# A four-layer kernel on one core: weights prepared in another order, the first image's values computed earlier, the second image's convolution inputs transformed once and kept in HBM

## The chip, the cores and the metric

The kernel runs on one core of a Trainium2 chip. The metric is the device time of one execution in microseconds. Of a core the reader needs TensorE (matmuls; a weight load goes before each), VectorE, ScalarE and GpSimd (elementwise work), and SyncE, which here only issues DMAs. They are PE, DVE, ACT, POOL and SP in the profile. Each engine takes its instructions in program order and they wait for each other by semaphores. TensorE writes to PSUM, which VectorE and ScalarE read; all else lies in SBUF, and DMAs move data between SBUF and HBM.

## What is computed

The input x is two images of 128 channels and 64 x 64 pixels, float32. Four layers follow each other:

```python
x = L0(x, ...)   # 1x1 embedding, two Mamba blocks (conv of 4 taps, scan over 4096 tokens, FFN), 1x1 out, + x
x = L1(x, ...)   # q, k, v = 3x3 convolutions of x; softmax(q.k / sqrt(C)) v over 4096 tokens; 1x1 out, + x
x = L2(x, ...)   # q, k, v = 1x1 convolutions; softmax(q.k) v; x + gamma * that
x = L3(x, ...)   # features at four scales, attention over the scales, layer norm, 1x1 fusion
```

The change touches the start of L0, and L1. Each image's L1 needs three 3x3 convolutions, for queries, keys and values, of the same input. They are done with a transform along the rows: out of six shifted views of a row, six combinations are made (they depend on the input alone), each is multiplied with a transformed weight, and four output columns come out of the six products.

## The kernel before

The activations of both images stay in SBUF as `xt`. L0 is cut into 32 items (image, block, chunk of 512 tokens), and each item into 32 slots. `slot` issues what belongs to the scan itself: the decay factors `da` (ACT, L377), the inputs of the scan `h` (DVE, `times_b`, L370), the scan (DVE, L388), the product with C (POOL, L391), the sum over states (PE, `y_pair`, L403), and the loads of `dtb` (`spread_dt`, SP, L359). `background` gives each slot its share of the matmuls and layer norms of the items before and after; its numbers are due slots, written by hand. Two rounds without a scan come first (items -2 and -1) and bring item 0 as far as the scan.

Before that stand the loads, all on SP in the order of the code: constants, eight chunks of the first image (L93), the embedding's weights, then for each of the two blocks its weights, the conv weights `cw` (L145, L146) and `wd`, then `raw`, the L1 convolution weights (L167), and the second image (L170). For each block VectorE makes `wu` (L152), and the table of decay rates `am` is made from `an` by four matmuls (L159) and 16 small copies (L162). The weights of L1 are transformed by `fold` (L172, ten VectorE operations for each of q, k and v), in slots 2, 10 and 18 of round -1, and stored to `ufold` in HBM. `spread_bc` (L327) sends an item's B and C through HBM (`dr`) and spreads them over partitions as `bb` and `cb`, all in slot 14.

L1 and L2 are one loop over `now`, 128 slots for each of four runs: L1 of both images, then L2 of both. A slot computes scores of 128 queries against 1024 keys (`score`, L725 on PE and L730 on DVE, which evicts them and takes maxima), and 14 slots later (`LAG`) four products of weights and values (`product`, L775). Between lie the exponentials (ACT, L740), a 32 x 32 block transpose (DVE, L755), and its rearrangement `pt<-tr`: 16 pieces a time, eight of them DMAs on SP (L766), four on ACT, four copies on POOL.

For L1, `inputs(r, cc)` (L587) makes the six combinations of a quarter of an image: twelve VectorE operations into `dlo` (four combinations, in the last part of the weight buffer `uw`) and `dhi` (two). `products_by` (L613) multiplies them with the transformed weights: 18 matmuls of 128 x 256, in six steps of three, one step for each combination. `outputs` (L634) makes the results: two ScalarE and nine VectorE operations. `beginning` runs the first image's queries (one quarter) and keys beside the last slots of L0; the string `beside` says how many of its steps stand in each slot. For the second image `keys` stands in front of its slot 0, and for both images `values` stands at the end of slot 13; both go through `chunks`, which calls `inputs` again for each quarter. `queries` of the other quarters stand at slot 30 of each 32, with `inputs` two operations a slot from slot 16 on. So each quarter of an image is transformed for queries, for keys and for values, apart from the quarters that are reused at once:

```python
pp = products(which)
ahead = inputs(r, cc + 1) if cc + 1 < NCC else []
for f in ahead[:8]:
    f()
outputs(*pp, [dst[:, i * QG : (i + 1) * QG] for i in range(4)], bias(r, which))
for f in ahead[8:]:
    f()
```

There is one `dlo` and one `dhi`: the next quarter's combination is written when the product that read the old one is done. L3, after the loop, is not touched.

Of the kernel before, what the change touches and what calls it, by code (L numbers as in the profile page):

```python
# [14 lines left out]
N = H * W  # L15
# [52 lines left out]
def tile_conv_seq(ctx: ExitStack, tc, x, consts, vecs, wemb, wlay, wconv, wdt, wqkv, wsmall, wms, out):  # L68
# [23 lines left out]
    for c in range(NCH):  # L92
        nc.sync.dma_start(xv(0, c), x[0, :, c * RPC : (c + 1) * RPC, :])  # L93

    ud = ctx.enter_context(tc.tile_pool(name="ufold", bufs=1, space=bass.MemoryType.DRAM))
    ufold = [ud.tile([P, 18, C], F32, name=f"ufold{k}") for k in range(3)]

# [16 lines left out]
    with tc.manual_schedule(), ExitStack() as s:  # L114
# [25 lines left out]
        wl, wu, wd, am = [], [], [], []  # L140
        for l in range(NL):
            w = wp.tile([P, NWL - DI], F32, name=f"wl{l}")
            nc.sync.dma_start(w, wlay[l][:, DI:])
            cw = sp.tile([P, KC + 1, DI], F32, name="cw", tag="h", bufs=5)
            nc.sync.dma_start(cw[:, :KC, :].rearrange("p k d -> p (k d)"), wconv[l : l + 1, :].to_broadcast([P, KC * DI]))  # L145
            nc.sync.dma_start(cw[:, KC, :], wlay[l][:, :DI])  # L146
            d = wp.tile([R, DI], F32, name=f"wd{l}")
            nc.sync.dma_start(d, wdt[l])

            u = wp.tile([P, KC, DI], F32, name=f"wu{l}")  # L150
            for k in range(KC):
                nc.vector.tensor_tensor(u[:, k, :], cw[:, KC, :], cw[:, k, :], ALU.mult)  # L152
            an = wp.tile([P, NJ * DS], F32, name=f"an{l}")
            nc.scalar.activation(an, vec[:, VEC[f"A_log{l}"] : VEC[f"A_log{l}"] + NJ * DS], AF.Exp)
            nc.vector.tensor_scalar(an, an, -1.0, None, ALU.mult)
            a = wp.tile([P, NJ, 4, 4], F32, name=f"am{l}")
            for g in range(4):
                pa = mm.tile([P, NJ, DS], F32, name="pa", tag="mm")
                nc.tensor.matmul(pa.rearrange("p j n -> p (j n)"), lhsT=four(g), rhs=an, start=True, stop=True)  # L159
                for q in range(4):  # L160
                    at = slice(32 * q, 32 * q + 32)
                    nc.vector.tensor_copy(a[at, :, g, :], pa[at, :, 4 * q : 4 * q + 4])  # L162
            wl.append(w), wu.append(u), wd.append(d), am.append(a)
        raws = []
        for which in range(3):
            raw = sp.tile([P, 3, 3, C], F32, name="raw", tag="h", bufs=5)
            nc.sync.dma_start(raw.rearrange("p y x c -> p (y x) c"), wqkv[:, which])  # L167
            raws.append(raw)
        for c in range(NCH):
            nc.sync.dma_start(xv(1, c), x[1, :, c * RPC : (c + 1) * RPC, :])  # L170
# [156 lines left out]
        def spread_bc(i):  # L327

            dr = dp.tile([2 * DS, CH], F32, name="dr", tag="dr")
            nc.sync.dma_start(dr, st[i]["dbl"][R:])  # L330
            for k in range(2):
                o = st[i]["bc", k] = sp.tile([P, 4, CH], F32, name=("bb", "cb")[k], tag=("bb", "cb")[k], bufs=2)
                for q in range(4):
                    src = dr[k * DS + 4 * q : k * DS + 4 * q + 4, :].rearrange("(o m) f -> o (m f)", o=1)
                    nc.sync.dma_start(o[32 * q : 32 * q + 32].rearrange("p m f -> p (m f)"), src.to_broadcast([32, 4 * CH]))
# [134 lines left out]
        def background(i):  # L470
# [14 lines left out]
            if has(n):  # L485
                at(0, pu_taps, n, 0, (0, 1)), at(1, pu_taps, n, 0, (2, 3)), at(2, pu_out, n, 0)
                at(3, pu_taps, n, 1, (0, 1)), at(4, pu_taps, n, 1, (2, 3)), at(5, pu_out, n, 1)
                at(13, xproj, n), at(14, xproj_out, n), at(14, spread_bc, n)
                at(15, dtproj, n, 0), at(16, dtproj, n, 1), at(17, soft_plus, n), at(18, dt_end, n)
# [5 lines left out]
            if i == -1:  # L495
                for k in range(3):
                    at(8 * k + 2, fold, k)
# [23 lines left out]
        def slot(i, todo, t_):  # L521
            t = i * NSL + t_
            g, m = divmod(t, 4)
            if m == 0 and 0 <= g + 3 < NG:
                spread_dt(g + 3)
            if m == 0 and 0 <= g + 1 < NG:
                spread_dtu(g + 1)
            if m == 0 and g % 2 == 1 and 0 <= g - 3 < NG:
                y_pair(g - 3)
            if 0 <= t < NT:  # L530
                scan(t)
            if 0 <= t + 4 < NT:
                decay(t + 4)
            if m == 3 and 0 <= g + 1 < NG:
                times_b(g + 1)
            for f, a in todo[t_]:
                f(*a)
# [75 lines left out]
        def products_by(which):  # L613
# [3 lines left out]
            for slot, dst in enumerate((pa[:, 2, :], pa[:, 0, :], pa[:, 3, :], pa[:, 1, :], pb[:, 0, :], pb[:, 1, :])):  # L617
                d = dlo[:, slot] if slot < 4 else sta["dhi"][:, slot - 4]
                for y in range(3):
                    rhs = d[:, y : y + 16, :].rearrange("p h j -> p (h j)")  # L620
                    lhsT = uw[:, where[which, slot // 3], 3 * (slot % 3) + y, :]
# [35 lines left out]
        def chunks(r, which, to):  # L657

            for cc in range(NCC):
# [6 lines left out]
                else:  # L666
                    pp = products(which)
                    ahead = inputs(r, cc + 1) if cc + 1 < NCC else []
                    for f in ahead[:8]:
                        f()  # L670
                    outputs(*pp, [dst[:, i * QG : (i + 1) * QG] for i in range(4)], bias(r, which))
                    for f in ahead[8:]:
                        f()
# [4 lines left out]

        def values(r):
            vt = sta["vt"] = sp.tile([P, N // P, C], F32, name="vt", tag="vt")  # L680
            vs = {}

            def turned(cc):
                for i in range(2):
                    pt = psa.tile([P, 4, P], F32, name="pvt", tag="acc")
                    for a in range(4):
                        at = (4 * i + a) * P
                        nc.tensor.transpose(pt[:, a, :], vs[cc][:, at : at + P], ident)
                    at = (2 * cc + i) * 4
                    nc.scalar.copy(vt[:, at : at + 4, :], pt)  # L690
# [129 lines left out]
        LO, HI = 0, 1  # L820
        def beginning():

            for which, half in ((0, LO), (0, HI), (1, LO)):
                load(which, half)
            for f in inputs(0, 0):
                f()
# [6 lines left out]
            k = sta["k"] = spa.tile([P, N], F32, name="k", tag="k")  # L833
            for cc in range(NCC):
                pp = yield from products_by(1)
                ahead = inputs(0, cc + 1) if cc + 1 < NCC else []
                for f in ahead[:8]:
                    f()
                at = cc * 4 * QG
                outputs(*pp, [k[:, at + i * QG : at + (i + 1) * QG] for i in range(4)], bias(0, 1))  # L840
# [5 lines left out]
        beside = '2111001000112111111011010000'  # L846
# [6 lines left out]
        for _ in steps:  # L853
            pass
        layers.close()
# [3 lines left out]
        for now in range(NALL + LAG + 10):  # L859
            r, u = divmod(now, NU)  # L860
            w = now % 8
            if now < NALL:
# [11 lines left out]
                if now >= 16 and r4 < B:  # L874
                    if v == 0:
                        ahead = inputs(r4, cc)
                    if v < 6:
                        for f in ahead[2 * v : 2 * v + 2]:
                            f()
                    if v == 14:  # L880
                        queries(r4, cc)
                        if r4 and cc == 0:
                            load(1, HI)
                score(r, u)
# [3 lines left out]
                elif u == 1:  # L888
                    load(2, LO), load(2, HI)
                    first = inputs(r, 0)  # L890
                elif 6 <= u < 12:
                    for f in first[2 * u - 12 : 2 * u - 10]:
                        f()
# [21 lines left out]
            if now < NALL and u == LAG - 1:  # L915
# [457 lines left out]
```

## Time and profile before

| | us |
|---|---|
| median of 3 runs | 5076.93 (5076.55 to 5080.12) |
| the profiled execution | 5077.7 |
| its span in the profile | 5075.9 |
| first scan starts | 84.94 |
| last scan ends, about | 2104 |
| first score of the attention (slot 0 of run 0) | 2189.1 |
| first score of slot 14 of run 0 | 2272.9 |
| first score of run 1 (L1, second image) | 2752.8 |
| first score of run 2 (L2, first image) | 3292.6 |
| last score | 4244.2 |

The times in the table are starts from the span's beginning. In the profile a line such as L725 is a line of the kernel; `out<-in` are the program's names; "idle before" is the time that the engine stood still just before an instruction, with what ended it. The granted clock is the share of TensorE's full clock: it is 1.00 or 0.50 at any moment, and a mean between them over a window.

The DMA issues that matter, from the page: each row is a group, with its queue, count, size and the median time from issue to landing.

| DMA | queue | count | KB | us |
|---|---|---|---|---|
| pt<-tr | SP | 2048 | 64 | 2.0 |
| dtb<-dt | SP | 1024 | 64 | 2.0 |
| bb<-dr | SP | 128 | 256 | 4.6 |
| cb<-dr | SP | 128 | 256 | 7.6 |
| uw<-ufold | SP | 14 | 576 | 3.7 |
| xt<-in_x | SP | 16 | 256 | 5.0 |
| xr<-in_x | SP | 16 | 256 | 2.9 |

### The profile page before, as it was taken

The numbers are of one execution on the slowest core, as the hardware profiler recorded it, in microseconds if no ns is written. First come the engines' busy times: TensorE is split into PE (matmuls) and PEld (weight loads), VectorE is DVE, ScalarE is ACT, GpSimd is POOL, SyncE is SP. The second block draws the span as 40 slices with busy tenths as digits, with TensorE's granted clock in tenths as the row PEclk, the third lists the DMA queues.
The fourth block names the chain that finished last, engine by engine and source line by source line (L and its number), as shares of the span: only waits on it lengthen the run. The fifth ranks groups of instructions, "written<-read, shape, count | busy, mean of one in ns | idle before, by whom it ended". The sixth has DMA issues, their size and how long they took to land.

```text
span 5075.9 us, 48999 instructions
## 1 busy us (share of the span) xinstructions
PE 4683.8 (92%) x14797; PEld 2250.9 (44%) x14797; DVE 4097.5 (81%) x4416; ACT 2366.9 (47%) x3221; POOL 2316.3 (46%) x1948
## 2 busy tenths in 40 slices
PE   5889999999988899889999999999999999999997
PEld 1222222222222222356666666666666666333332
DVE  5999999999999999788888878667766775667775
ACT  4677777777777777522222222333333332323332
POOL 2777776766777777413332233233333332322331
PEclk8898889988999989899999999999999999999998
DMA  5333333333333333124443344444444443000000
GB/s 149 72 69 68 70 71 70 72 69 68 69 70 68 72 72 71 46 54 102 105 102 84 77 104 103 118 97 111 111 100 99 112 111 77 5 5 7 7 7 7
DMA packets 237016, 373.86 MB, mean 74 GB/s; under 512 B 88000, under 2 KB 88400, under 8 KB 228432
## 3 DMA queue, kind: packets, MB, share of 16 engines
q1 hardware_dynamic: 187600, 303.55, 25.8%
q10 hardware_dynamic: 49152, 67.17, 5.8%
q8 instruction: 118, 1.93, 0.2%
q14 instruction: 146, 1.20, 0.1%
HBM read 92.18 MB, written 9.83 MB: 20 GB/s over the span
## 4 chain that ended last, share of the span: by engine, by line
PE 47%; POOL 21%; DVE 13%; issue 11%; DMA 3%; ACT 3%; SPq 2%; ACTq 0%; DVEq 0%; POOLq 0%
POOL h L391 16%; PE po L775 13%; PE pq L725 13%; DVE tr L755 3%; DMA pt<-tr 2%; PE pf L1060 2%; SPq L766 2%; PE py L403 2%; PE pqkv L1087 2%; PE pu L292 1%; PE pw L1146 1%; POOL dtu L351 1%; PE pfus L1211 1%; POOL z L414 1%; PE psc L1111 1%
## 5 line engine op out<-in xcount | busy, mean ns | idle before, releaser
L762 POOL COPY pt<-tr 32x512 f32<-32x512 f32 x1024 | 656.1, 641 | 1468.2 <-DVE tr L755 738.8
L388 DVE TENSOR_TENSOR_SCAN h<-da,carry,h 128x512 f32<-128x512 f32 x1024 | 1241.4, 1266 | 60.4 <-ACT da L377 31.6
L391 POOL TENSOR_TENSOR h<-h,cb 128x2048 f32<-128x2048 f32 x256 | 1161.1, 4536 | 20.8 <-POOL carry L390 0.2
L725 PE MATMUL pq<-k,q 128*128 128x512 f32 x2048 | 965.1, 594 | 11.2 <-DVE sc L730 8.8
L775 PE MATMUL po<-pt,vt 128*128 128x256 f32 x4096 | 967.5, 380 | 2.4 <-DMA pt<-tr 2.4
L740 ACT ACTIVATE sc<-sc,nm 128x2048 f32<-128x2048 f32 x256 | 510.6, 1995 | 937.2 <-DVE nm L736 641.7
L730 DVE TENSOR_SCALAR_CACHE_REDUCE sc<-pq 128x1024 f32<-128x1024 f32 x512 | 624.9, 1222 | 359.8 <-PE pq L725 337.9
L775 PEld LDWEIGHTS po<-pt,vt 128*128 128x128 f32 x4096 | 780.5, 191 | 293.9 <-issue 211.1
L377 ACT ACTIVATE da<-dtb,am 128x512 f32<-128x512 f32 x1024 | 681.7, 684 | 222.1 <-DVE h L388 210.6
L755 DVE STREAM_TRANSPOSE tr<-sc 128x2048 f32<-128x2048 f32 x256 | 591.6, 2311 | 65.8 <-DMA pt<-tr 60.5
L370 DVE TENSOR_TENSOR h<-bb,pdu 128x2048 f32<-128x2048 f32 x256 | 581.7, 2272 | 77.4 <-PE py L403 29.3
L403 PE MATMUL py<-h,sel 128*32 128x512 f32 x2048 | 511.5, 643 | 1.6 <-POOL h L391 1.6
L725 PEld LDWEIGHTS pq<-k,q 128*128 128x128 f32 x2048 | 384.5, 191 | 289.5 <-issue 247.1
L364 PE MATMUL pdu<-dtu,fsel 128*128 128x512 f32 x512 | 326.5, 724 | 101.9 <-DVE h L370 101.8
L403 PEld LDWEIGHTS py<-h,sel 128*32 128x32 f32 x2048 | 115.7, 118 | 415.9 <-issue 408.9
L292 PE MATMUL pu<-xn,wu 128*128 128x512 f32 x512 | 246.2, 615 | 3.0 <-ACT xn L282 2.1
L364 PEld LDWEIGHTS pdu<-dtu,fsel 128*128 128x128 f32 x512 | 96.2, 215 | 308.3 <-DVE h L370 187.6
L390 POOL COPY carry<-h 128x4 f32<-128x4 f32 x256 | 47.5, 185 | 388.1 <-DVE h L388 383.5
L1153 DVE TENSOR_TENSOR ov<-v,pw 128x2048 f32<-128x2048 f32 x64 | 146.2, 2285 | 68.5 <-PE pw L1146 68.5
L1087 PE MATMUL pqkv<-f,ws 128*128 128x512 f32 x384 | 189.7, 619 | 3.0 <-DVE prod L1104 2.3
L1157 POOL TENSOR_TENSOR ov<-ov 128x2048 f32<-128x2048 f32 x16 | 72.6, 4537 | 257.6 <-DVE ov L1153 257.6
L351 POOL TENSOR_TENSOR dtu<-dt,u 128x1024 f32<-128x1024 f32 x32 | 75.0, 2345 | 189.7 <-ACT dt L345 189.7
(241 smaller groups left out, 5344.1 us busy)
## 6 DMA issues: line engine op xcount, KB each, us to landing
pt<-tr SPq DMA_DIRECT2D x2048, 64.0 KB, 2.0
dtb<-dt SPq DMA_DIRECT2D x1024, 64.0 KB, 2.0
pt<-tr ACTq DMA_DIRECT2D x1024, 64.0 KB, 2.2
bb<-dr SPq DMA_DIRECT2D x128, 256.0 KB, 4.6
cb<-dr SPq DMA_DIRECT2D x128, 256.0 KB, 7.6
uw<-ufold SPq DMA_DIRECT2D x14, 576.0 KB, 3.7
xt<-in_x SPq DMA_DIRECT2D x16, 256.0 KB, 5.0
xr<-in_x SPq DMA_DIRECT2D x16, 256.0 KB, 2.9
```

Of the source, the lines that this page charges most:

```text
L364: nc.tensor.matmul(pdu, lhsT=four(s_ % 4), rhs=st[i]["dtu"][:, s_ // 4, :], start=True, stop=True)
L370: nc.vector.tensor_tensor(h, st[i]["bc", 0], pdu.unsqueeze(1).to_broadcast([P, 4, CH]), ALU.mult)
L377: nc.scalar.activation(da, st[i]["dtb", s_], AF.Exp, scale=am[items[i][1]][:, j, gg, m : m + 1])
L388: nc.vector.tensor_tensor_scan(h[:, m, :], da, h[:, m, :], carries[b, l][:, j, gg, m : m + 1], ALU.mult, ALU.add)
L391: nc.gpsimd.tensor_tensor(h, h, st[i]["bc", 1], ALU.mult)
L403: nc.tensor.matmul(py[r : r + 32, :], lhsT=sel, rhs=st[i]["h", s_ + k][:, m, :], start=(m == 0), stop=(m == 3), tile_position=(0, r),)
L725: nc.tensor.matmul(pq[:, i, :], lhsT=sta["q", r, grp][:, it * P : (it + 1) * P], rhs=sta["k"][:, at : at + CH], start=True, stop=True)
L730: nc.vector.tensor_scalar(dst, pq, 1.0, None, ALU.mult, ALU.max, accum_out=sta["mx"][:, c2 : c2 + 1])
L740: nc.scalar.activation(sc, sc, AF.Exp, bias=nm, scale=scale, accum_out=sm[:, hh : hh + 1])
L755: nc.vector.transpose(tr, sta.pop(("sc", r, blk, hh)).rearrange("p (t r f) -> p r t f", r=NB, f=32))
L762: nc.gpsimd.tensor_copy(dst, src)
L775: nc.tensor.matmul(sta["po", r, grp], lhsT=sta["vt"][:, jt, :], rhs=rhs, start=(jt == 0), stop=(jt == N // P - 1))
```

## The change

It has three parts.

The start: one chunk of the first image is loaded, then the first block's weights with `cw` ahead, then the other chunks and the second block. `prepare` makes a block's `am` ahead of its `wu`; that of the second block moves to slot 7 of round -1, the loads of `raw` and of the second image are issued in slot 1 of it, and the three folds stand in slots 8, 9 and 10. `cb` is spread in slot 22 instead of 14. The first `spread_dtu` and `times_b` get slots 19 and 26 of that round.

The values of the first image: `beginning` computes them beside the keys, from the same combinations, quarter by quarter, with their weights in a buffer of their own (`uv`). They are turned into `vt` in slots 0 to 3 of run 0 (`turned`). The block at slot 13 remains for the second image alone.

The second image: during run 0 its quarters are transformed in slots 32, 64 and 96 (and the first one from slot 112 on, as before), and `keep` stores each to HBM, `dkept`. For keys, values and queries of run 1, `fetch` loads a quarter back in three DMAs on SP, one for each two combinations, in place of the twelve operations.

```diff
-    for c in range(NCH):
-        nc.sync.dma_start(xv(0, c), x[0, :, c * RPC : (c + 1) * RPC, :])
+    def load_x(b, c):
+        nc.sync.dma_start(xv(b, c), x[b, :, c * RPC : (c + 1) * RPC, :])
...
+    dkept = [ud.tile([P, 6, 18 * 16], F32, name=f"dkept{k}") for k in range(4)]
...
-        wl, wu, wd, am = [], [], [], []
-        for l in range(NL):
+        load_x(0, 0)
+        wl, wu, wd, am, cws = [], [], [], [], []
+
+        def load_layer(l):
+            cw = sp.tile([P, KC + 1, DI], F32, name="cw", tag="h", bufs=5)
+            nc.sync.dma_start(cw[:, KC, :], wlay[l][:, :DI])
+            nc.sync.dma_start(cw[:, :KC, :].rearrange("p k d -> p (k d)"), wconv[l : l + 1, :].to_broadcast([P, KC * DI]))
+            cws.append(cw)
             w = wp.tile([P, NWL - DI], F32, name=f"wl{l}")
...
-            cw = sp.tile([P, KC + 1, DI], F32, name="cw", tag="h", bufs=5)
-            nc.sync.dma_start(cw[:, :KC, :].rearrange("p k d -> p (k d)"), wconv[l : l + 1, :].to_broadcast([P, KC * DI]))
-            nc.sync.dma_start(cw[:, KC, :], wlay[l][:, :DI])
...
-            u = wp.tile([P, KC, DI], F32, name=f"wu{l}")
-            for k in range(KC):
-                nc.vector.tensor_tensor(u[:, k, :], cw[:, KC, :], cw[:, k, :], ALU.mult)
+            wl.append(w), wd.append(d)
+
+        def prepare(l):
             an = wp.tile([P, NJ * DS], F32, name=f"an{l}")
...
-            wl.append(w), wu.append(u), wd.append(d), am.append(a)
+
+            u, cw = wp.tile([P, KC, DI], F32, name=f"wu{l}"), cws[l]
+            for k in range(KC):
+                nc.vector.tensor_tensor(u[:, k, :], cw[:, KC, :], cw[:, k, :], ALU.mult)
+            wu.append(u), am.append(a)
...
+        def load_rest():
...
+            for c in range(NCH):
+                load_x(1, c)
+
+        load_layer(0)
+        load_x(0, 1)
+        prepare(0)
+        for c in range(2, NCH):
+            load_x(0, c)
+        load_layer(1)
...
-        def spread_bc(i):
...
+        def spread_bc(i, k):
+
+            if k == 0:
+                st[i]["dr"] = dp.tile([2 * DS, CH], F32, name="dr", tag="dr")
+                nc.sync.dma_start(st[i]["dr"], st[i]["dbl"][R:])
+            dr = st[i]["dr"]
...
-                at(13, xproj, n), at(14, xproj_out, n), at(14, spread_bc, n)
+                at(13, xproj, n), at(14, xproj_out, n), at(14, spread_bc, n, 0), at(22, spread_bc, n, 1)
...
             if i == -1:
+                at(1, load_rest), at(7, prepare, 1)
                 for k in range(3):
-                    at(8 * k + 2, fold, k)
+                    at(8 + k, fold, k)
+                at(19, spread_dtu, 0), at(26, times_b, 0)
...
-            if m == 0 and 0 <= g + 1 < NG:
+            if m == 0 and 1 <= g + 1 < NG:
...
-            if m == 3 and 0 <= g + 1 < NG:
+            if m == 3 and 1 <= g + 1 < NG:
...
-        def products_by(which):
+        def keep(cc):
+            nc.sync.dma_start(dkept[cc][:, :4, :], dlo.rearrange("p s y j -> p s (y j)"))
+            nc.sync.dma_start(dkept[cc][:, 4:, :], sta["dhi"].rearrange("p s y j -> p s (y j)"))
+
+        def fetch(cc):
+            dhi = sta["dhi"] = spa.tile([P, 2, 18, 16], F32, name="dhi", tag="d")
+            for k, d in enumerate((dlo[:, :2], dlo[:, 2:], dhi)):
+                nc.sync.dma_start(d.rearrange("p s y j -> p s (y j)"), dkept[cc][:, 2 * k : 2 * k + 2, :])
+
+        def products_by(which, w=None):
...
-                    lhsT = uw[:, where[which, slot // 3], 3 * (slot % 3) + y, :]
+                    lhsT = uw[:, where[which, slot // 3], 3 * (slot % 3) + y, :] if w is None else w[:, 3 * slot + y, :]
...
                     pp = products(which)
-                    ahead = inputs(r, cc + 1) if cc + 1 < NCC else []
-                    for f in ahead[:8]:
-                        f()
+                    if cc + 1 < NCC:
+                        fetch(cc + 1)
                     outputs(*pp, [dst[:, i * QG : (i + 1) * QG] for i in range(4)], bias(r, which))
-                    for f in ahead[8:]:
-                        f()
...
+        vs = {}
+
+        def turned(cc):
+
+            for i in range(2):
+                pt = psa.tile([P, 4, P], F32, name="pvt", tag="acc")
+                for a in range(4):
+                    at = (4 * i + a) * P
+                    nc.tensor.transpose(pt[:, a, :], vs[cc][:, at : at + P], ident)
+                at = (2 * cc + i) * 4
+                nc.scalar.copy(sta["vt"][:, at : at + 4, :], pt)
...
+        once = ExitStack()
+        uv = once.enter_context(tc.tile_pool(name="ato", bufs=1, reuse_waits="tile", side="right")).tile([P, 18, C], F32, name="uv")
+
...
+            nc.sync.dma_start(uv, ufold[2])
...
+            sta["vt"] = spa.tile([P, N // P, C], F32, name="vt", tag="vt")
             for cc in range(NCC):
                 pp = yield from products_by(1)
+                at = cc * 4 * QG
+                outputs(*pp, [k[:, at + i * QG : at + (i + 1) * QG] for i in range(4)], bias(0, 1))
+                if cc % 2 == 0:
+                    both = spa.tile([P, 2, 4 * QG], F32, name="vs", tag="tr", bufs=2)
+                vs[cc] = both[:, cc % 2, :]
+                pp = yield from products_by(2, uv)
                 ahead = inputs(0, cc + 1) if cc + 1 < NCC else []
                 for f in ahead[:8]:
                     f()
-                at = cc * 4 * QG
-                outputs(*pp, [k[:, at + i * QG : at + (i + 1) * QG] for i in range(4)], bias(0, 1))
+                outputs(*pp, [vs[cc][:, i * QG : (i + 1) * QG] for i in range(4)], bias(0, 2))
                 for f in ahead[8:]:
                     f()
...
-        beside = '2111001000112111111011010000'
+        beside = '21110010001121111110110111111111111111'
...
                 if now >= 16 and r4 < B:
-                    if v == 0:
+                    if v == 0 and r4 and cc:
+                        fetch(cc)
+                    elif v == 0:
                         ahead = inputs(r4, cc)
-                    if v < 6:
+                    if v < 6 and not (r4 and cc):
                         for f in ahead[2 * v : 2 * v + 2]:
                             f()
+                    if v == 6 and r4 and cc == 0:
+                        keep(0)
                     if v == 14:
                         queries(r4, cc)
                         if r4 and cc == 0:
                             load(1, HI)
+
+                if r == 0 and u >= 32:
+                    v = u % 32
+                    if v == 0:
+                        other = inputs(1, u // 32)
+                    if v < 6:
+                        for f in other[2 * v : 2 * v + 2]:
+                            f()
+                    if v == 6:
+                        keep(u // 32)
...
-                elif u == 1:
+                elif u == 1 and r:
                     load(2, LO), load(2, HI)
-                    first = inputs(r, 0)
-                elif 6 <= u < 12:
-                    for f in first[2 * u - 12 : 2 * u - 10]:
-                        f()
+                    fetch(0)
...
-            if now < NALL and u == LAG - 1:
+            if now < NCC:
+                turned(now)
+            if r and now < NALL and u == LAG - 1:
                 values(r)
```

## The prediction

> **What bounds the kernel now.** I read the profile in this order: the page's engine shares, then a table of busy time by stretch of the span, then the timelines of the three places that the change touches. The page says that no engine is the limit everywhere:
>
> ```profile
> PE 4683.8 (92%) x14797; PEld 2250.9 (44%) x14797; DVE 4097.5 (81%) x4416; ACT 2366.9 (47%) x3221; POOL 2316.3 (46%) x1948
> ```
>
> So the stretches decide. In each row: window, its length, then busy us (and instructions) of PE, PEld, DVE, ACT, POOL, the granted clock, the DMA share, GB/s.
>
> ```profile
> 0.00:85.00 85.00, 36.76 (x60) 13.00 (x60) 27.51 (x81) 22.79 (x32) 8.66 (x22) 0.89 0.68 185
> 85.00:2104.00 2019.00, 1810.81 (x4595) 551.52 (x4594) 1882.52 (x1403) 1467.06 (x2076) 1427.33 (x671) 0.90 0.31 69
> 2104.00:2189.00 85.00, 72.88 (x255) 45.08 (x253) 50.66 (x95) 25.39 (x36) 9.35 (x4) 0.98 0.15 48
> 2189.00:2273.00 84.00, 66.02 (x236) 43.09 (x235) 74.95 (x132) 19.95 (x29) 15.37 (x20) 0.94 0.27 69
> 2273.00:2710.00 437.00, 434.40 (x1583) 296.21 (x1582) 349.62 (x533) 122.44 (x134) 148.31 (x224) 1.00 0.45 103
> 2710.00:2753.00 43.00, 37.30 (x165) 30.34 (x164) 41.05 (x79) 7.03 (x12) 3.48 (x4) 1.00 0.18 47
> 2800.00:2845.00 45.00, 40.52 (x187) 33.12 (x187) 40.87 (x81) 8.17 (x19) 4.70 (x7) 0.96 0.24 62
> ```
>
> What to see: the scan stage (second row) is VectorE's at 93%. The loop of the first attention (fifth row) is TensorE's at 99.4%, so a VectorE operation taken out of that loop buys almost nothing. Time is loose in three places only: the start, where no engine is half busy and DMA is; the 169 us from the last scan to slot 14 of the first image (third and fourth rows); the key and value blocks of the second image (last two rows), where TensorE stops for VectorE.
>
> **Part 1, the start.** Today the first scan begins at 84.94.
>
> ```profile
> 19.58 1.43 DVE L152 TENSOR_TENSOR wu<-cw 128x256 f32<-128x256 f32 x4 [15.18 <-DMA cw<-in_wlay]
> ...
> 29.31 2.05 PE L217 MATMUL pe<-xt,we 128*128 128x512 f32 x2
> ...
> 74.45 16.03 SPq L359 DMA_DIRECT2D dtb<-dt  x19
> ...
> 84.16 1.30 ACT L377 ACTIVATE da<-dtb,am 128x512 f32<-128x512 f32 x2 [8.21 <-DMA dtb<-dt]
> 84.94 4.81 DVE L388 TENSOR_TENSOR_SCAN h<-da,carry,h 128x512 f32<-128x512 f32 x4 [1.20 <-ACT da L377]
> ```
>
> VectorE waits 15 us for cw, which stands behind all eight x loads on SP; the decay table (an, am) follows it and the first embedding follows that, at 29.3. The change loads one x chunk, then cw, and makes the decay table first. It needs only constants landed at 3.5 to 3.7, so an is done at about 4.6, and the table-to-embedding distance (26.25 to 29.28 for the second layer's table now) puts the embedding at 7.7; the x chunk, behind 0.5 MB of constants, lands near 6.2 at the 1.17 us a chunk at which chunks land now. The chain moves forward 21.6 us.
>
> Not all of it arrives. The second layer's table (exp 0.25, 3.7 us of matmuls and copies) and its wu (1.43) now stand ahead of the three folds, 15.3 us on VectorE (45.76 to 61.02 today). They start when u is out, near 36, so the folds end near 56.6. SP takes the last fold's store before dr, so dr waits for the fold although its data is ready near 45. From there: dr 1.6, four bb loads (today 71.98 to 75.6, 7.0 after the first issue), so times_b, which is now ahead of ln_scale on VectorE, runs 65.9 to 68.2, ln_scale to 68.9. dtb, issued right after bb instead of after cb and a fold, lands near 67; exp 0.69 fits. First scan at 69: **gain 16** (10 if the folds start late, 20 if dr isn't held up). The cover for the late cb: POOL needs it 4.9 after the first scan, and four loads of 1.2 us bring it at about 72, before 73.9. Later items have eight slots of about 2 us more than cb's 7.6 us; nothing there.
>
> **Part 2, the first image's values move into the tail.** The values block costs 44.9 us between two scores (slots 13 and 14) for 34.4 us of matmuls, and the 12 operations of "first" in slots 6 to 11 cost VectorE 8.3 us in a stretch where it is the limit (75 of 84 us). Both go. The matmuls (72 of 0.43 us, 30.9) move into the tail, which ends its key products at 2186.4. There TensorE has these idle stretches:
>
> ```profile
> 2145.45 1.56 PE L622 MATMUL pb<-dhi,uw 128*128 128x256 f32 x6 [0.80 <-DVE dhi L608]
> 2148.16 1.98 PE L436 MATMUL ph<-x,wl 128*128 128x512 f32 x4 [1.15 <-ACT x L282]
> ...
> 2157.15 5.40 PE L448 MATMUL pf<-hid,wl 128*128 128x512 f32 x8 [4.00 <-ACT hid L440]
> ...
> 2172.93 2.86 PE L622 MATMUL pb<-dhi,uw 128*128 128x256 f32 x12 [1.57 <-DVE dhi L608]
> 2175.99 5.42 PE L622 MATMUL pa<-uw 128*128 128x256 f32 x24 [0.20 <-DVE uw L601]
> 2183.72 2.86 PE L622 MATMUL pb<-dhi,uw 128*128 128x256 f32 x12 [2.31 <-DVE dhi L608]
> ```
>
> With value products between the key products, the transform of the next chunk (7.4 us) and the key outputs (4.0) run beside 7.7 us of value matmuls, and the wait for gelu is filled. The named waits (10.0), and 1.7 lost when the clock halves after the 4.0 us wait (5.40 instead of 3.70), can all go: value products end at 2186.4 + 30.9 - 11.7 = 2205.6. First score 2.7 later (as today) at 2208.3, less 1 for partly overlapped outputs. Slots 0 to 13 then take 38.9 - 8.3 = 30.6, plus slot 13's own score and transpose, 3.6: slot 14 at about 2241.5. Its transposes (3.4 us of TensorE) fit in slots 0 to 3, where TensorE has 1.7 us of work for a slot of 2.5. Today slot 14 starts at 2272.9. **Gain 31.** If no wait is filled, the 11.7 come back: 19. The new load uv (1.18 MB) waits for ffn_down at 2115 on SP, with xr behind it; at the start's 185 to 250 GB/s it lands by 2123, and xr is needed at 2124.8: no cost, or 1 us.
>
> **Part 3, transform once and fetch.** Of 22 transforms 11 go, 81 us of VectorE. What counts is where. In slots 6 to 11 of the second image I take 1.2 us (its first 13 slots last 47.5, those of the next attention, with no transform, 46.8, plus a wait of 0.98 for dg that moves). In the loops, 32 slots with a transform have 2.5 us of slack against 1.1 without; the three transforms added to the first image's loop pay that, the three taken from the second's give it back: 0. The keep stores (0.9 MB each) have SP and DMA at 45% as cover.
>
> The blocks: keys of the second image take 37.9 us for 30.9 of matmuls (waits 7.0), values 6.0 more than theirs. With fetch, each third of the buffer is refilled as soon as the two products that read it are done, so it has 5.1 us before its next use. A 295 KB load lies between xr (256 KB, 2.9 us) and uw (576 KB, 3.7): 3 us, hidden. Not the first one of a block: on SP it stands behind the eight pt loads of the turn just before (8 x 0.63), issued 7.8 us after the block began; the second chunk waits 3.0 us in keys, 3.7 in values, where that turn is later.
>
> Such a hole may halve the clock. [...] But the trace has one after a hole of 2.0 us:
>
> ```profile
> 2826.46 4.54 PE L622 MATMUL pb<-dhi,uw 128*128 128x256 f32 x12 [2.02 <-DVE dhi L608]
> ```
>
> 4.54 for 2.86, so 1.7. I go by the row and charge it in both blocks: keys 7.0 - 3.0 - 1.7 - 0.3 = 2.0, values 6.0 - 3.7 - 1.7 - 0.2 = 0.4. [...] **Gain 2.4**; between a loss of 2 and a gain of 10.
>
> **Sum.** 16 + 31 + 1.2 + 2.4 = 50.6. The profiled execution took 5077.7 (span 5075.9 and 1.8 around it), so 5027.1; the median of the runs shown, 5076.93, is 0.8 below it. I predict **5027**.
>
> **Rivals.**
> 1. Chance 0.2: the tail isn't filled; VectorE's outputs and transforms set its pace and the 11.7 stay: 5027 + 12 = 5039. For it: all four chunks' dhi waits are VectorE's today. Against: 7.7 us of matmuls now stand between.
> 2. Chance 0.11: fetches are late each time, by 4 us (they queue behind pt on the same DMA engines). Six times 4, with a cold stretch of 1.7 in each block, is 27.4 against 13 saved: blocks lose 14 where I have a gain of 2.4: 5044.
> 3. Chance 0.05, slower than before: the same place with the clock. If each of the six fetches came only after its whole chunk (7.6 us, cb's landing) and the array then ran the next chunk at half clock (7.7 more), 92 us would go for 13 saved: 5077.7 - 48.2 - 13 + 92 = 5108. It decides from about 12 us a fetch ((48.2 + 13 + 10) / 6). Against it: each third is released by itself.
> 4. Chance 0.02: gains and losses cancel within 10 us, or the moved work only shifts the end.
>
> My forecast has 0.62. **Range**: gains of 20 + 36 + 3 + 10 give 5009, of 10 + 19 + 0 - 2 give 5051; both ends at once are unlikely, so 5008 to 5046, which takes in rivals 1 and 2. Faster by more than 0.2% (10 us, about what a measurement of this kernel can tell from no change): 0.93; within: 0.02; slower: 0.05.
>
> **What would show it.** First scan near 69, with dr issued just after the last fold's store; first score near 2190 of the new span (2207 less 16); no 45 us pause at slot 13; in the two blocks one wait of 3 to 4 us for an uw or dhi load, at the second chunk, not three; the loops' 32-slot stretches unchanged at 122.9. Wrong would be: dr issued near 45 (start better), value products with waits for dhi between them (rival 1), waits for fetches at every chunk (2, 3).

## The result, and the profile after

The changed kernel took 5031.26 us (median of 4 runs, 5029.0 to 5033.83), the kernel before 5078.52 beside it: ratio 0.9907, 95% interval 0.9891 to 0.9923. The forecast was 5027. The profiled execution took 5032.79, its span 5031.0, so 44.9 us shorter than the span before.

The page's row of engines, after:

```profile
PE 4671.6 (93%) x14797; PEld 2244.9 (45%) x14797; DVE 4024.3 (80%) x4284; ACT 2367.4 (47%) x3221; POOL 2309.9 (46%) x1948
```

VectorE has 73 us less to do (11 of its 22 transforms are gone) and TensorE the same number of matmuls. As before, the stretches tell more. The same table by stretch (window, length, then busy us and instructions of PE, PEld, DVE, ACT, POOL, granted clock, DMA share, GB/s): start, scan stage, tail, slots 0 to 13 of the first image, its loop, the second image's keys block and values block.

```profile
0.00:73.50 73.50, 36.21 (x59) 12.63 (x60) 31.58 (x81) 23.26 (x32) 8.99 (x22) 0.81 0.75 206
73.50:2093.00 2019.50, 1810.38 (x4595) 550.52 (x4594) 1882.97 (x1404) 1466.92 (x2074) 1427.48 (x671) 0.90 0.31 69
2093.00:2197.00 104.00, 101.14 (x406) 73.11 (x405) 66.20 (x131) 28.92 (x45) 9.58 (x4) 1.00 0.12 40
2197.00:2234.50 37.50, 30.67 (x94) 15.03 (x94) 30.94 (x49) 16.38 (x21) 10.03 (x17) 1.00 0.32 80
2234.50:2675.00 440.50, 435.34 (x1574) 293.57 (x1573) 372.28 (x569) 122.44 (x134) 158.94 (x228) 1.00 0.46 116
2675.00:2714.00 39.00, 35.95 (x163) 30.61 (x162) 19.59 (x42) 7.03 (x12) 2.43 (x4) 1.00 0.47 139
...
2762.00:2808.00 46.00, 42.04 (x192) 34.61 (x192) 19.22 (x41) 7.34 (x16) 2.43 (x4) 0.96 0.35 103
```

The scan stage is what it was. In the tail TensorE is now busy 101 of 104 us, 73 of 85 before: the value products filled it. In the first image's loop VectorE went from 350 to 372 us and the loop from 437.0 to 440.5. The start is 11.5 us shorter although no engine has much less to do there.

Told by the starts of single instructions (first and last scan, VectorE's evictions of the scores), the span divides like this; the last columns are experiments told below. "Run 0" and "run 1" are the first attention of the two images, "slots 0 to 14" goes from the first score to that of slot 14, "to run 2" to the first score of the second attention.

| us | before | changed | forecast gain | gain | no_keep | fold_in_two_places | all_together |
|---|---|---|---|---|---|---|---|
| to the first scan | 84.9 | 73.5 | 16 | 11.5 | 72.7 | 63.0 | 61.6 |
| scans | 2016.7 | 2017.4 | 0 | -0.7 | 2016.5 | 2016.3 | 2017.1 |
| last scan to first score | 87.5 | 106.1 | } 31 | } 27.9 | 106.2 | 106.1 | 106.1 |
| run 0, slots 0 to 14 | 83.9 | 37.3 | | | 37.3 | 37.3 | 37.4 |
| run 0, slots 14 to 127 | 437.1 | 440.8 | 0 | -3.7 | 436.5 | 440.1 | 430.0 |
| keys block | 42.7 | 39.0 | 2.0 | 3.7 | 42.7 | 37.8 | 37.6 |
| run 1, slots 0 to 13 | 47.3 | 45.3 | 1.2 | 2.0 | 47.3 | 45.3 | 45.3 |
| values block | 44.8 | 44.5 | 0.4 | 0.3 | 44.9 | 40.3 | 40.5 |
| run 1, slot 14 to run 2 | 447.6 | 444.2 | 0 | 3.5 | 446.2 | 443.8 | 443.2 |
| rest | 1783.3 | 1782.9 | 0 | 0.4 | 1782.7 | 1781.7 | 1783.3 |

Three terms carry the miss: the start 4.5 and the values 3.1 too large, the keys block 1.7 too small. The start has a spread of its own: five of the ten kernels have its code unchanged (the changed kernel, start_only, no_keep, fetch_on_act, one_op_a_slot), and their first scans stand at 73.5, 72.7, 72.7, 70.8 and 72.6.

### The profile page after: what moved, and what is told of

Same layout as the page of the kernel before. It is cut to its first block, busy times and chain, and to the rows that moved or that the text cites. A ratio compares the mean times of both kernels' runs of the same rounds, so it can differ in the third digit from the quotient of the medians.

```text
span 5031.0 us, 48923 instructions
## 1 busy us (share of the span) xinstructions
PE 4671.6 (93%) x14797; PEld 2244.9 (45%) x14797; DVE 4024.3 (80%) x4284; ACT 2367.4 (47%) x3221; POOL 2309.9 (46%) x1948
## 3 DMA queue, kind: packets, MB, share of 16 engines
q8 instruction: 118, 1.93, 0.2%
## 4 chain that ended last, share of the span: by engine, by line
PE 49%; POOL 24%; issue 12%; DVE 9%; ACT 2%; DMA 2%; SPq 1%; ACTq 0%; DVEq 0%; POOLq 0%
POOL h L410 19%; PE po L804 15%; PE pq L754 15%; PE pa L652 2%; PE pf L1113 2%; DVE tr L784 2%; PE pqkv L1140 2%; POOL dtu L370 1%; PE pw L1199 1%; POOL z L433 1%; PE pb L652 1%; PE pfus L1264 1%; PE psc L1164 1%; PE po L1220 1%; DVE prod L1157 1%
## 5 line engine op out<-in xcount | busy, mean ns | idle before, releaser
L1210 POOL TENSOR_TENSOR ov<-ov 128x2048 f32<-128x2048 f32 x16 | 72.6, 4536 | 257.7 <-DVE ov L1206 257.7
```

## What the trace shows of the start and of the blocks

VectorE's timeline of the changed kernel in the start, the three stretched operations of the folds and what waits behind them (start, length, engine, line, operation, out<-in):

```profile
49.37 0.56 DVE L201 SCALAR_TENSOR_TENSOR ulo<-raw,uhi 128x384 f32<-128x384 f32 x1
49.96 2.62 DVE L202 SCALAR_TENSOR_TENSOR uhi<-raw,uhi 128x384 f32<-128x384 f32 x1
...
54.01 1.40 DVE L196 TENSOR_SCALAR ulo<-ulo 128x384 f32<-128x384 f32 x1
...
56.03 1.65 DVE L198 SCALAR_TENSOR_TENSOR ulo<-raw,ulo 128x384 f32<-128x384 f32 x1
...
70.61 2.29 DVE L389 TENSOR_TENSOR h<-bb,pdu 128x2048 f32<-128x2048 f32 x1 [9.95 <-DMA bb<-dr]
```

GpSimd's timeline in the same microseconds:

```profile
49.83 2.34 POOL L370 TENSOR_TENSOR dtu<-dt,u 128x1024 f32<-128x1024 f32 x1 [28.37 <-ACT dt L364]
53.93 1.25 POOL L274 TENSOR_TENSOR nt<-nt,ve 1x512 f32<-1x512 f32 x1 [1.76 <-ACT nt L269]
56.02 1.25 POOL L279 TENSOR_TENSOR rs<-rs,nt 1x512 f32<-1x512 f32 x1 [0.83 <-ACT nt L275]
```

Each stretched operation began within 0.13 us of a GpSimd product and ended 0.2 to 0.4 after it. The other instances of L202, L196 and L198 take 0.56, 0.36 and 0.56, so 4.2 us were lost. SyncE's queue shows who passed that on:

```profile
60.69 0.32 SPq L206 DMA_DIRECT2D ufold<-uhi  x1
61.10 0.41 SPq L349 DMA_DIRECT2D dr<-dbl  x1
63.77 1.71 SPq L354 DMA_DIRECT2D bb<-dr  x4
```

dr left right behind the last fold's store, as forecast, but at 61.1 instead of 57, and took 2.65 us to land, not 1.6.

TensorE in the second image's keys block and then its values block (in brackets the idle time before and what ended it):

```profile
2682.25 2.75 PE L652 MATMUL pb<-dhi,uw 128*128 128x256 f32 x12
2688.06 5.42 PE L652 MATMUL pa<-uw 128*128 128x256 f32 x24 [3.05 <-DMA uw<-dkept]
2693.31 2.75 PE L652 MATMUL pb<-dhi,uw 128*128 128x256 f32 x12
...
2766.15 2.75 PE L652 MATMUL pb<-dhi,uw 128*128 128x256 f32 x12
2772.08 7.10 PE L652 MATMUL pa<-uw 128*128 128x256 f32 x24 [3.17 <-DMA uw<-dkept]
2779.02 2.75 PE L652 MATMUL pb<-dhi,uw 128*128 128x256 f32 x12
```

One wait in each block, at the second chunk. After the one of 3.05 the next group runs at full clock (5.42), after the one of 3.17 it takes 7.10, 1.76 more than the 5.34 of a warm group.

## Experiments: the parts by themselves

**start_only**: the kernel before with the start's edits (part 1), nothing else.

> The kernel before with the new start alone (part 1). Theory A, terms add up: the first scan moves as in the changed kernel, from 84.9 to 73.5, and the scan stage keeps its 2019 us, so the run is 10.7 to 11.5 us shorter than before: about 5067.5. Rival: cb spread at slot 22 and the smaller bursts on SP also change the scan stage or the tail, so that the start alone is worth 16 or more, or 5 or less.

5064.3 us (13 runs) against 5076.4, ratio 0.9977 (0.9969 to 0.9985): 12.1 us. First scan at 72.7, scan stage 2016.8, tail and run 0 as before. The rival falls: the start is a term of its own.

**no_keep**: the changed kernel, with keys, values and queries of the second image transformed anew.

```diff
-                    if cc + 1 < NCC:
-                        fetch(cc + 1)
+                    ahead = inputs(r, cc + 1) if cc + 1 < NCC else []
...
-                if r == 0 and u >= 32:
...
-                    fetch(0)
+                    first = inputs(r, 0)
```

> The changed kernel with part 3 undone: the second image is transformed again for keys, values and queries, nothing is stored or fetched; start and values stay. Theory A: part 3 is worth 6 us net (first image's loop pays 3.5, keys block gives 3.7, second image 5.8), so this run is 6 slower than the changed kernel and 38 to 39 faster than before: about 5039; the loops' 32-slot stretches go back to 122.9. Rival: the 81 us of VectorE that part 3 saves are worth 12 us or more (5045 or above), or nothing (5031).

5034.91 against 5076.4, ratio 0.9923 (0.9909 to 0.9936). Against start_only this is 29.4 us for the values. What part 3 is worth is less than the intervals of two ratios can part, but its stretches show it (table above): run 0 pays 4.3 (436.5 to 440.8), keys give 3.6, slots 0 to 13 of run 1 2.0, values 0.4, the rest of run 1 2.1: 3.7 net for 48 us of VectorE (4072.0 here, 4024.3 in the changed kernel). Of the 11 transforms that are gone 7 belong to part 3; the other 4 went with the first image's values, and the expectation's 81 us counted them in. The 32-slot stretches of run 0 are back at 122.9 and 123.2. Theory A, smaller than told; the rival of 12 falls, that of nothing by the stretches alone.

## Experiments: the start

**folds_behind_dr**: only SyncE's order changes.

```diff
-                    at(8 + k, fold, k)
+                    at(15 + k, fold, k)
```

> The changed kernel with the three folds issued in slots 15 to 17 in place of 8 to 10; no engine but SP changes its order: dr and the four bb loads now stand before the six stores of the folds. Theory A, dr was held on SP by the last fold's store: dr is issued some 10 us earlier, bb lands before the folds end near 60.7, times_b starts then (70.6 before), the first scan is near 66 to 67, 7 us gained: about 5024. Rival B, the stretched folds and the dtb loads behind them set the start: dtb lands last and the first scan stays at 72 to 73, 5030.

First scan at 68.8: 4.7 of the 7 us. The profiled execution took 5024.2, but the median is 5029.88 (5024.23 to 5032.21; ratio 0.9909, 0.9896 to 0.9923), so the times alone don't show it. VectorE's timeline tells where the rest stayed:

```profile
46.97 0.56 DVE L198 SCALAR_TENSOR_TENSOR ulo<-raw,ulo 128x384 f32<-128x384 f32 x1
55.19 0.68 DVE L199 SCALAR_TENSOR_TENSOR uhi<-raw 128x384 f32<-128x384 f32 x1 [7.67 <-DMA ufold<-ulo]
...
63.41 2.29 DVE L389 TENSOR_TENSOR h<-bb,pdu 128x2048 f32<-128x2048 f32 x1
```

dr left at 45.2 and times_b no longer waits for bb. But the first fold's store, issued behind four bb loads, landed late, and the second fold needs its buffer: 7.7 us. dtb, behind the last store (issued from 63.8), then set the first scan. The hold on SyncE was real; two others came in its place. No fold operation is stretched by more than 0.13 here, since GpSimd's products ran while VectorE stood still.

**first_dtu_on_vectore**: one GpSimd product taken away.

```diff
-            nc.gpsimd.tensor_tensor(w["dtu"], w["dt"], w["u"], ALU.mult)
+            (nc.gpsimd if i else nc.vector).tensor_tensor(w["dtu"], w["dt"], w["u"], ALU.mult)
```

> The changed kernel with the first chunk's product dt*u on VectorE, behind the folds, in place of GpSimd. Theory A, a VectorE operation that meets a GpSimd one waits for it to end: the fold operation of 2.62 us goes back to 0.56, the folds end about 2 us earlier, and the two stretched by the normalisation's products (1.40 and 1.65) stay. As dr is held by the last fold's store, the first scan is 2 us earlier, near 71. Rival B, the stretch has another cause (a store landing, an input not yet there): an operation of 2.6 stays at that place and the first scan at 73.

VectorE's timeline at the same place, with the operation that now has the product behind it:

```profile
48.55 0.56 DVE L202 SCALAR_TENSOR_TENSOR uhi<-raw,uhi 128x384 f32<-128x384 f32 x1
...
52.97 1.56 DVE L201 SCALAR_TENSOR_TENSOR ulo<-raw,uhi 128x384 f32<-128x384 f32 x1
...
55.96 1.36 DVE L370 TENSOR_TENSOR dtu<-dt,u 128x1024 f32<-128x1024 f32 x1
```

The operation of 2.6 us is gone, and one of the two shorter stretches with it (the second of the two small products fell beside operations that did not wait). The folds took 16.3 us from first to last instead of 19.5, began 1.4 earlier, and the first scan is at 69.1. Part of that is the spread of the start: counted from the first fold, the first scan comes after 29.4 us here and after 31.4 to 32.5 in the five kernels with the product on GpSimd, so 2 to 3 us are the edit's. Theory A expected 2; rival B falls. The one execution took 5021.78, 11.0 less than the changed kernel's profiled one, but 5.1 of these lie behind the first score of run 2, which the edit doesn't touch.

**fold_in_two_places**: the first fold before dr, the others behind dtb, and the first fetch of each block on ScalarE's queue.

```diff
-                    at(8 + k, fold, k)
+                    at((8, 21, 22)[k], fold, k)
...
-                        fetch(cc + 1)
+                        fetch(cc + 1, nc.sync if cc else nc.scalar)
```

> The changed kernel with the folds in slots 8, 21 and 22 (SP: the first fold's stores, dr, bb, dtb, then the other folds' stores and cb), and with only the first fetch of each block on ScalarE's queue. Theory A, with folds behind dr the first scan was set by two things, the second fold's wait of 7.7 us for its buffer, whose store landed behind bb, and by dtb behind the last store: both go, the last fold ends at 58 to 61, then times_b 2.3, ln_scale 0.7, first scan at 63 to 65 (73.5 in the changed kernel, 68.8 with all folds behind dr). Rival B: the second fold still waits for a buffer behind the bb loads, first scan 67 or later. Blocks: keys 37.7 (39.0 in the changed kernel), values 40.5 (44.5), as ScalarE's queue is free of the later fetches.

5013.32 us against 5078.63, ratio 0.9870 (0.9855 to 0.9885). SyncE's queue:

```profile
45.77 0.33 SPq L206 DMA_DIRECT2D ufold<-uhi  x1
47.75 0.32 SPq L349 DMA_DIRECT2D dr<-dbl  x1
49.37 1.71 SPq L354 DMA_DIRECT2D bb<-dr  x4
51.18 2.50 SPq L378 DMA_DIRECT2D dtb<-dt  x4
```

dr leaves 13.4 us earlier than in the changed kernel; no fold waits for a buffer; times_b follows the last fold with no wait (60.12) and the first scan is at 63.0. Now the folds on VectorE are the limit of the start, the stretches by GpSimd (4.1 us) included.

## Experiments: blocks and loops

**fetch_on_act**: all fetches on ScalarE's queue.

```diff
-                nc.sync.dma_start(d.rearrange("p s y j -> p (s y j)"), dkept[cc][:, 2 * k : 2 * k + 2, :])
+                nc.scalar.dma_start(d.rearrange("p s y j -> p (s y j)"), dkept[cc][:, 2 * k : 2 * k + 2, :])
```

> The changed kernel with the fetches issued on ScalarE's queue in place of SP's. Theory A, the one stall in each block is the fetch standing behind eight pt loads on SP: both stalls go (3.05 in keys, 3.17 in values and the 1.76 of half clock after it), 8 us gained: about 5023. Rival B, the transfer itself is slow beside the pt transfers, or the outputs' copies on ScalarE now wait behind the fetches: 0 to 2 us gained, or a stall at every chunk and a loss of some 6.

5023.89 against 5076.4, ratio 0.9900 (0.9886 to 0.9913). Keys block 38.5 (39.0), values block 40.5 (44.5). TensorE in the two blocks:

```profile
2683.01 5.42 PE L652 MATMUL pa<-uw 128*128 128x256 f32 x24 [1.78 <-DMA uw<-dkept]
...
2696.27 2.86 PE L652 MATMUL pb<-dhi,uw 128*128 128x256 f32 x12
...
2765.44 5.42 PE L652 MATMUL pa<-uw 128*128 128x256 f32 x24 [0.89 <-DMA uw<-dkept]
```

Both theories hold in part. The waits shrink by 1.3 and 2.3 but stay: on ScalarE's queue too the fetch follows four pt loads (it left at 2679.20) and lands 3.7 us later. The half clock behind the wait in values is gone. In keys the later fetches hold ScalarE's copies for the outputs, which costs back 0.7; with only the first fetch moved (fold_in_two_places) keys take 37.8. Why it lands after 3.7 there, and after 3.1 on SyncE's queue, was not tried apart. The forecast of 5023 was met partly by luck: of the 8 us between the profiled executions the blocks gave 4.6, and 2.7 lie in the start, whose code is the same.

**one_op_a_slot**: two edits in different stretches.

```diff
-                    if v < 6:
-                        for f in other[2 * v : 2 * v + 2]:
-                            f()
-                    if v == 6:
+                    if v < 12:
+                        other[v]()
+                    if v == 12:
...
-            if now < NCC:
-                turned(now)
+            if 3 <= now < 3 + NCC:
+                turned(now - 3)
```

> The changed kernel with two edits in stretches that don't touch: the transforms in the loops issue one operation a slot over twelve slots instead of two over six, and the value transposes stand in slots 3 to 6 of the first image instead of 0 to 3. Theory A, in the loops a transform costs time only because two of its operations make VectorE the limit in three pairs of slots: the first image's two 32-slot stretches with two transforms go from 124.4 and 124.7 to about 122 (121.5 without any transform), 10 us or so over the loop. Rival: VectorE's work in the stretch counts, however it is spread, and they stay at 124.5. Transposes: theory A, they cost 2.8 us because slots 0 to 4 are TensorE's; in slots 5 and 6 TensorE waits for VectorE, so slots 0 to 14 go from 37.3 to about 36. Rival: their copies stand behind the exponentials on ScalarE and hold TensorE, 39 or more.

5034.2 against 5078.63, ratio 0.9912 (0.9896 to 0.9929): a large gain and a larger loss. Slots 32 to 96 of run 0 went from 249.0 to 242.9, to the tenth what they take in run 1 with no transform at all; all of slots 14 to 127 gave 10.4. The loop never paid for VectorE's time, only for two operations in one slot. The transposes lost 12.0 (slots 0 to 14: 49.25 for 37.28). TensorE's timeline there, then ScalarE's:

```profile
2200.64 1.04 PE L714 MATMUL pvt<-kc,vs 128*128 128x128 f32 x8
2201.51 1.88 PE L754 MATMUL pq<-k,q 128*128 128x512 f32 x4
2207.09 1.40 PE L714 MATMUL pvt<-kc,vs 128*128 128x128 f32 x8 [3.69 <-ACT vt L716]
...
2218.85 1.97 PE L714 MATMUL pvt<-kc,vs 128*128 128x128 f32 x8 [4.62 <-ACT vt L716]
...
2204.49 1.99 ACT L769 ACTIVATE sc<-sc,nm 128x2048 f32<-128x2048 f32 x1
2206.47 1.05 ACT L716 COPY vt<-pvt 128x512 f32<-128x512 f32 x2
...
2218.21 1.07 ACT L716 COPY vt<-pvt 128x512 f32<-128x512 f32 x2 [9.10 <-DMA pt<-tr]
```

TensorE waits for ScalarE's copies. The first time they stand behind the exponentials, as the rival has it. The second time ScalarE has nothing to compute: its copies stand behind the four pt loads that it issues itself, and these wait for VectorE's block transpose, which ends at 2215.4. The run also gives the cost in the changed kernel: its first three slots take 1.2, 2.2, 1.7 us without transposes, 1.7, 2.6, 2.6 with them.

**all_together**: the changed kernel with folds in two places, the first chunk's dt*u on VectorE between them, the first fetch of a block on ScalarE's queue, and one transform operation a slot.

> The changed kernel with what helped in the runs above: folds in slots 8, 21 and 22, the first chunk's product dt*u on VectorE between the second and third fold (its spread to slot 23), the first fetch of each block on ScalarE's queue, and one transform operation a slot in the loops; the transposes stay in slots 0 to 3. Theory A, the terms add up: first scan at about 60.5 (63.0, less the 2.6 us that the folds stood still beside GpSimd's product), loops 10.4 shorter as with one operation a slot, blocks as with the first fetch on ScalarE's queue: 5013.3 - 10.4 - 2.6 = about 5000, ratio 0.985. Rival: an earlier start and a loop without slack meet something else (cb, a fetch that the loop's stores hold, the transposes' transfers), and less than 7 of the 13 us arrive: 5006 or more.

5000.61 us against 5075.22, ratio 0.9851 (0.9835 to 0.9868), first scan 61.6, run 0 from slot 14 in 430.0. As forecast; the rival of 5006 falls. It is faster than both kernels: 74.6 us off the kernel before, where the change took 47.3. The first scan is 1.1 later than told: in fold_in_two_places GpSimd's dt*u held a fold operation for 2.0 us, not 2.6, and on VectorE the product itself takes 1.1 between the folds, which the expectation left out.

## Why the prediction came out as it did

**Right in the mechanisms, 5.7 us too hopeful in the sum (44.9 saved between the profiled spans, 50.6 forecast).** Point by point:

- *Start, forecast 16, measured 11.5.* The chain moved forward by 21.5 as worked out (first embedding at 7.80 for 29.31), the folds began at the forecast place (after wu, 41.2), dr stood behind the last fold's store. The term that was mis-sized is "the three folds, 15.3 us on VectorE (45.76 to 61.02 today)": at the new place they took 19.5, because they now run beside GpSimd's first products (first_dtu_on_vectore, and folds_behind_dr, where none is stretched by more than 0.13). That is 4.2 too much. The second is dr's landing, 2.65 for 1.6; smaller terms give some 0.7 back. I moved an operation to a new place and took its duration from the old one without asking what runs there on the other engine. The rows show the price: 2.62 for 0.56 beside a product of 2.34, and each of the three operations that waited had started second, 0.13, 0.08 and 0.01 us behind GpSimd's.
- *Values, forecast 31, measured 27.9.* The tail filled as forecast (first score at 2197.0, with the 10.8 by which the last scan is earlier 2207.8; forecast 2207.3; one wait of 1.58 left); rival 1 falls. The 8.3 us of transform operations in slots 6 to 11 all came out: slots 5 to 13 took 30.5 and take 21.9. The failed step is "its transposes fit in slots 0 to 3, where TensorE has 1.7 us of work for a slot of 2.5": the slots there lasted 1.1 to 2.2, nearly all of it TensorE's own, so transposes added 2.7; slot 13 took 4.2 for 3.6 (rows of the first five slots below the list).
- *Loops, forecast 0, measured -3.7 and +3.5.* That the first image pays what the second gets back was right. What I read as a price of VectorE's work was a price of two operations in a slot.
- *Second image.* Slots 0 to 13 gave 2.0 for 1.2. In both blocks the one wait is where and nearly as long as forecast (3.05 for 3.0, 3.17 for 3.7), and every later fetch is in time: rivals 2 and 3 fall. The prediction charged half clock in both blocks, on one row of before (4.54 for 2.86 after a hole of 2.02). It came in values (7.10) and not in keys (5.42), so keys gave 3.7, not 2.0. But in first_dtu_on_vectore and one_op_a_slot the keys block met half clock too, after holes of 2.79 and 2.92 (7.11 in both), and took 40.5 and 40.6. So that keys gave 3.7 in the profiled execution and not some 2.2 is luck, and without it the sum would have been 1.5 further off. One row of before could not tell which block would pay; what the traces show of it stands in the last section.
- *VectorE.* The "81 us of VectorE" that the prediction puts under part 3 takes in the four transforms of the first image's values. Part 3 saves 48 (no_keep). No term of the sum rests on it, as each was taken from a stretch.

The first five slots of the first image, before and after, in the columns of the table by stretch:

```profile
2189.13:2197.59 8.46, 8.07 (x20) 3.39 (x19) 6.39 (x14) 1.79 (x1) 0.00 (x0) 1.00 0.00 0
2197.03:2208.23 11.20, 11.20 (x45) 6.28 (x44) 6.47 (x12) 5.44 (x9) 0.00 (x0) 1.00 0.00 0
```

## What to carry to other kernels

When an operation moves, price it by what runs beside it at its new place: what other engine's operations can hold it (here 4.2 us beside GpSimd's products), what stands behind it in a DMA queue (dr left 13.4 us earlier with two folds moved behind it), and whose buffer it frees (a wait of 7.7 us in folds_behind_dr). Work that fits an engine's average slack can still cost time if it comes two at a time; one operation a slot made the transforms of the first image's loop free (slots 32 to 96 in 242.9 us for 249.0). A stage that is "not VectorE's" is not loose if it is TensorE's own (the transposes added 2.7 us to slots of 1.1 to 2.2): look at each slot's length before putting work there.

## What the runs showed of the hardware

**The clock after a hole.** Over the ten traces, with holes of 1.5 us and more before the products of the attention's convolutions: of those up to 1.91 us none was followed by half clock; of 12 between 1.93 and 2.33, five; of 8 between 2.79 and 3.20, six. A hole of 2.31 did it in the keys block of no_keep, ones of 2.32 and 2.33 did not in the keys block of before. The length between 1.9 and 3.2 doesn't decide; each costs 1.7 us when it happens (7.10 for 5.42 in the changed kernel, 4.54 for 2.86 in before).

What parts them in these traces is where the hole lies. In every trace the granted clock changes only at points of a raster of 3.41 us: in the changed kernel 77 stretches of half clock begin, from 38.17 to 5031.87, each a whole number of times 3.413 after the first, to within 0.01; in before 82, as closely. Between 2100 and 3200 us the ten traces have 3201 steps of the raster at full clock. In the 18 that half clock followed TensorE stood still for 1.93 us or more, in the other 3183 for at most 1.95 (before: 4 of 316 steps, with 1.98 to 3.41, the others at most 1.95; the changed kernel: 1 of 320, with 3.17, the others at most 1.91). The hole of 3.05 in keys was cut by a point of the raster into 1.91 and 1.14; that of 3.17 in values lay within one step. These are the steps of the changed kernel (window, length, PE's busy us, granted clock, DMA share, GB/s):

```profile
2683.50:2686.91 3.41, 1.50 (x7) 1.00 0.59 140
2686.91:2690.33 3.42, 2.27 (x11) 1.00 0.56 213
...
2768.83:2772.25 3.42, 0.25 (x2) 1.00 0.78 224
2772.25:2775.66 3.41, 3.41 (x9) 0.50 0.19 72
```

Half clock for one step of 3.41 is the 1.7 us lost. Who doesn't know where a hole will lie can price it as a chance. An estimate from the 1.93 and the 3.41, for that stretch alone: about three in four for a hole of 3.0 us, about one in two for 2.0 to 2.3, none below 1.9. In the scan stage it doesn't hold: of 60 falls to half clock in the changed kernel 46 follow steps in which TensorE stood still for less than 1.9 us, two of them (at 543.34 and 1813.10) steps in which it was busy for all 3.41, and that was not looked into.

**Which operations wait for GpSimd.** The fold operations with two inputs in SBUF waited: L195 (2.51 for 0.55 in fold_in_two_places), L198 (1.65 for 0.56 in the changed kernel), L199 (1.62 for 0.55 in one_op_a_slot), L201 (1.56 for 0.56 in first_dtu_on_vectore), L202 (2.62 for 0.56 in the changed kernel). So did the contiguous one-input L196 (1.40 for 0.36 in the changed kernel) and L200 (1.38 for 0.36 in all_together). The one-input L203 and L204 took 0.54 to 0.55 in every timeline, even where they lay beside GpSimd's product, as in fetch_on_act (GpSimd busy from 48.32 to 50.86):

```profile
48.57 0.54 DVE L203 TENSOR_SCALAR uhi<-raw 128x384 f32<-128x384 f32 x1
49.03 0.54 DVE L204 COPY uhi<-raw 128x384 f32<-128x384 f32 x1
49.49 1.78 DVE L195 TENSOR_TENSOR ulo<-raw 128x384 f32<-128x384 f32 x1
```
